# Norms of the first Mamba blocks placed inside the attention stage, with other buffer counts, fewer transfers and new planner offsets

## The chip, the cores and the metric

The kernel runs on one core of one Trainium2 chip. The metric is the device time of one execution in microseconds (us). The engines are named as in the profile: PE (matrix products and transposes), PEld (its weight loads), DVE (vector), ACT (activations and scaled copies), POOL (general vector work, indirect transfers), SP (transfer queue).

## The reference

The input x is two images of 256 channels and 48 x 48 pixels. Three layers follow each other.

```python
# layer 0: 7x7 neighbourhood attention (4 heads of 64) beside a depthwise convolution
q, k, v = c1x1(x, Wq), c1x1(x, Wk), c1x1(x, Wv)
att = softmax(einsum('bdn,bdkn->bnk', q * 64**-0.5, unfold(pad_reflect(k)) + unfold_pe))
out_att = einsum('bnk,bdkn->bdn', att, unfold(pad_reflect(v)))
...
hid = relu(dwconv(x, w1)); oc = dwconv(hid, w2)
x = rate1 * out_att + rate2 * out_conv
# layer 1: per-token norm, a Mamba mixer over all 2304 tokens of an image, output projection
# then: router over 8 experts, the best two of them for each token, experts of 256 -> 1024 -> 256
```

The kernel also applies group norms to the images ahead of layer 0. In layer 1 every token is normalized over its 256 channels; the kernel does this in blocks of 384 tokens.

## The kernel before

Both images stay in the on-chip memory as x[0] and x[1], two halves of 128 channels by 2304 pixels. The work comes in three stages, each a `Flow`: operations are handed to a planner with a key, an engine, a cost in ns, the operations that they need, the buffers that they take and release (`room` gives how many of each there are), and a due time. The planner ranks ready operations by due time, the length of what follows, and an offset for each kind of operation (the tables `LEAD0` and `LEAD1`; in stage one a kind has one offset for image 0, "-", and one for image 1, "+"). It emits them in that order, and each engine runs its own list in that order. "queue" stands for transfers that SP issues.

**Attention (`layer0`).** Each image is normalized into planes xp[b, h] (`group_norm`). Products with Wk (`keys`, L702), Wq (`queries`, L659) and Wv (`values`, L749) read the planes. The values go to DRAM (`store`), and from there into a key table vtab that has the borders mirrored (`spread`, `ends`). A group of 16 rows of the table is written by nine transfers: three of up to 22 columns, and six of a single column each (L772, L775). An image has 18 blocks of 8 x 16 pixels. For block c (`block`): scores (L811, PE), minimum against the mask (L827, DVE), exponentials (L838, ACT), transposes (L846, PE), copies pt (L852, ACT), the product with val (L868, PE), which has been loaded from vtab (L911). The reciprocals of the sums are widened into rx (L889, POOL), transposed (L894, PE) and copied into rb (L900, ACT); a product on DVE (L882) and an add into x (L878) end the block. Beside that run the convolutions: nine taps each for two passes (L565, L577 on DVE, L597, L626 on ACT, accumulating transfers on POOL, L638), gathered into x by L603.

**Mamba (`mamba`).** Twelve blocks of 384 tokens, six of each image. For block k, `norms` transposes the tokens (L1048, PE), copies them into t (L1058, ACT), takes moments (L1051, L1054, DVE), does the inverse root and its products on POOL (L1089 to L1102, the power at L1093), writes the residual back to x (L1107, ACT) and normalizes t in place (L1114, ACT). `project_block` then turns t back (L1137, PE) into xn (L1144, ACT), sets or copies three columns at the head of xn (L1150, L1152), and multiplies by the weights `win` (L975, PE): 128 x 387 for the convolution, 128 x 384 for the gate, 128 x 16 for dt and gate logits. Chunks of 128 tokens run through the scan and the output projection, the router groups them, and rows are scattered to a table by POOL (L1738). The first experts' tiles are computed early in this stage.

**Experts (`experts`).** Tiles of up to 256 rows go through both matrices of an expert (L2144, L2187), and the results are added to DRAM by indirect transfers (L2154). Last the sums are read back, transposed and written (`results`).

Of the kernel before, what the change touches and what calls it, by code (L numbers as in the profile page):

```python
# [31 lines left out]
F32 = mybir.dt.float32  # L32
# [42 lines left out]
TR = 256  # L75
CAP = B * N
# [156 lines left out]
class Kernel:  # L233
# [49 lines left out]
    def begin_flow(self, pool, room, pace, lead, half=0):  # L283

        self.m, self.pace, self.flow, self.tiles, self.last = pool, pace, Flow(room, lead, half), {}, {}
# [8 lines left out]
    def op(self, c, key, engine, cost, make, *needs, **kw):  # L294
        if engine == "POOL":
            make = partial(self.on_pool, key[0] == "put", make)
        self.flow.add(key, engine, cost, make, needs, due=c * self.pace, **kw)
# [19 lines left out]
    def small_tile(self, name, key, shape, dtype=F32, bufs=4):  # L317
        t = self.tiles[name, key] = self.small.tile(shape, dtype, tag=f"m{name}", name=name, bufs=bufs)
        return t

    def large_tile(self, name, key, shape, pool=None):
        slot = self.flow.slot[name, key]
        t = self.tiles[name, key] = (pool or self.m).tile(shape, F32, tag=f"{name}{slot}", name=name)
        return t

# [12 lines left out]
    def layer0(self, ctx):  # L338
# [5 lines left out]
        room = dict(bank=2, banks=3, q=2, prob=3, pt=4, val=3, vout=2, hid=2, place=2, ct=2, cg=2, rb=2, ot=1, rx=2)  # L344
        self.begin_flow(self.pool("att", 1, ctx), room, self.PACE0, self.LEAD0, NBQ * self.PACE0)
        self.xp = {(b, h): wts.tile([P, H, W], F32, name=f"xp{b}{h}") for b in range(B) for h in range(NH)}
# [3 lines left out]
        for b in range(B):  # L350
            self.group_norm(b)
            for g in range(-(-H // KG)):
                self.keys(b, g)
            for rb in range(NRB):
                self.queries(b, rb)
            for pair in range(N // (2 * P)):
                self.values(b, pair)
            self.convolutions(b)
            for i in range(NBQ):
                self.block(b * NBQ + i)  # L360
        self.run_flow()

# [370 lines left out]
    def values(self, b, pair):  # L733
# [27 lines left out]
        def spread():  # L761
# [4 lines left out]
            for cb in range(NCB):  # L766
                c0, c1 = max(0, cb * QC - PAD), min(W, (cb + 1) * QC + PAD)
                at = c0 - (cb * QC - PAD)
                nc.sync.dma_start(strips[cb, rows, at : at + c1 - c0, :], src[r0:r1, c0:c1, :])
                for j in range(PAD):  # L770
                    if cb == 0:
                        nc.sync.dma_start(strips[cb, rows, j : j + 1, :], src[r0:r1, PAD - j : PAD - j + 1, :])  # L772
                    if cb == NCB - 1:
                        col = QC + PAD + j
                        nc.sync.dma_start(strips[cb, rows, col : col + 1, :], src[r0:r1, W - 2 - j : W - 1 - j, :])  # L775
# [11 lines left out]
        self.op(c, ("vs", key), "queue", 4500, store, ("vc", key), uses=[("vout", key)])  # L787
        if done:
            self.op(c, ("vt", (b, group)), "queue", 10000, spread, *[("vs", (b, p)) for p in range(pair - 2, pair + 1)])
# [3 lines left out]
    def block(self, c):  # L793
# [25 lines left out]
        for h in range(NH):  # L819
            key = (c, h)  # L820

            def least(h=h, key=key):
                if h == 0:
                    self.small_tile("top", c, wide)
# [8 lines left out]
            def exps(h=h):  # L833
                if h == 0:
                    self.small_tile("den", c, wide)
# [83 lines left out]
        "Wk-": -2983844, "Wq-": -2364428, "Wv-": 1379269, "add+": 4672699, "add-": -218998,  # L919
        "bkp-": -329119, "bq8-": -347513, "bv1-": -2824447, "c1+": -2744499, "c1-": 604148,  # L920
        "c2+": -3568598, "c2-": -4067744, "c3+": -4192745, "c3-": 1206176, "ca+": -316981,
        "ca-": 1533923, "cd+": -6915146, "cd-": 3124390, "copy+": 5626139, "copy-": -1580149,
        "cp+": -1382670, "cp-": -1157911, "cst-": 2506359, "exps+": -3895413, "exps-": -4687265,
        "g2+": 3892042, "g2-": -3058028, "ga-": -6766507, "gneg-": 557252, "gs-": -9485502,
        "ka+": -2261356, "ka-": 4495797, "kb+": 754107, "kb-": 2128455, "kk+": -355426, "kk-":
        95965, "least+": -852851, "least-": -3615547, "line-": -4892590, "mix+": 3379755,
        "mix-": 5352508, "norm+": -2808328, "norm-": -848702, "place+": 2730989, "place-":
        4548299, "q+": 272749, "q-": 1258423, "qp+": -359879, "qp-": 5581, "rc+": -1347439,
        "rc-": 1599623, "rden+": -1647488, "rden-": -463776, "relu+": 7308982, "relu-": 4577314,
        "row-": -5624948, "rstd-": 3924930, "rt+": 965921, "rt-": -18691, "rx+": -6558515,  # L930
        "rx-": -3369941, "score+": 3504231, "score-": 2190083, "sw+": -848532, "turn+":
        -1205935, "turn-": 84883, "v+": 110806, "v-": 10811, "val+": 448065, "val-": 3685159,
        "vc+": -519738, "vc-": -124400, "ve+": 2263088, "ve-": -7064210, "vec-": -4450165,
        "vs+": -1985565, "vs-": -5738649, "vt+": 5333280, "vt-": 1460046, "w2r-": -7510221,
        "win-": 4743570, "winw+": -1186160, "woutc+": 774295, "woutd+": 1826874, "woute+":
        -6026117, "woutt+": -512791, "woutw+": -8672401, "wp-": -1208524, "wv1-": -2064644,
        "x-": -4900900, "xp-": -8007513,
# [39 lines left out]
    def mamba(self, ctx):  # L977
# [32 lines left out]
        "al": -290978, "begin": 28518, "btt": 903929, "ct": -258969, "cum": 138318, "cv": 4160,  # L1010
        "decayed": 600184, "dg": 29752, "dt": 100727, "dx": -4156, "ea": -277213, "ebegin":
        -102059, "ed": -105474, "efetch": 1438, "eg": 26883, "eown": 41250, "eplan": -216891,
        "eput": -260074, "er": 287202, "es": -882262, "et": -610518, "etoken": -82312, "eu":
        -375317, "ew": 321735, "eweight": -249839, "ex": -22495, "ext": 45975, "from": 77621,
        "g10": -530705, "g5": 86017, "g6": 266930, "g8": 619114, "g9": -284332, "ge": -53696,
        "gm": -98648, "gmrs": 207272, "grs": 157083, "gsm": -121187, "gsw": -603090, "gw":
        -597259, "head": -444384, "kap": 244339, "keep": -167944, "lg": -74165, "mm": 175579,
        "mo": -45640, "mrs": 201963, "msw": -491777, "mt": -64622, "n2": -327525, "nt": 132852,
        "number": -110107, "out": -69798, "pg": -24798, "place": 60192, "ps": 382782, "pst":
        95326, "put": -322183, "py": 88837, "rd": 122406, "rg": -214014, "row": 58828, "rs":  # L1020
        216632, "rs1": -164526, "s0": 477684, "s4": 611494, "s5": 133846, "scores": -252255,
        "silu": -226005, "silub": 88047, "silux": 101715, "sm": 481060, "spread": -243362, "sq":
        -69048, "sr": -36881, "ss": -35615, "st": -60640, "state": -249719, "stats": -437860,
        "su": -1199, "tap": 131999, "tb": 14763, "tc": 292305, "tx": 467979, "u2": -251857,
        "xc": 488195, "xd": 18280, "xo": 475933, "xt": 66896, "xw": 407174, "ya": 7940, "yb":
        -85276, "yi": -88374, "yz": -140873, "z": -15500,
    }

    def norms(self, k):
# [5 lines left out]
        def op(name, engine, cost, make, *needs, **kw):  # L1035
            self.op(k * NJ, (name, k) if isinstance(name, str) else name, engine, cost, make, *needs, **kw)

        for j in range(NJ):
# [3 lines left out]
            def turn(j=j, at=at, cols=cols):  # L1042
                if j == 0:
                    self.large_tile("t", k, [P, NJ, C])
# [8 lines left out]
            def moments(j=j, at=at):  # L1053
                nc.vector.bn_aggr(T["mv", k][:, j, :], T["lst", at])  # L1054

            op(("nt", at), "PE", 220, turn, ("nt", (k, j - 1)) if j else None,
               takes=[("bank", ("nt", at))] + ([("t", k)] if j == 0 else []))
            op(("tc", at), "ACT", 380, lambda j=j, at=at: nc.scalar.copy(T["t", k][:, j, :], T["bank", ("nt", at)][:, :C]),  # L1058
               ("nt", at), uses=[("bank", ("nt", at))])
            self.chain(k * NJ, ("stats", at), [("DVE", 410, stats), ("DVE", 180, moments)], ("tc", at))  # L1060
# [27 lines left out]
        self.chain(k * NJ, ("n2", k), [  # L1088
# [9 lines left out]
        self.chain(k * NJ, ("kap", k), [  # L1098
# [5 lines left out]
        ), *[("stats", (k, j)) for j in range(NJ)])  # L1104
# [16 lines left out]
    def project_block(self, k):  # L1121


        nc, T, win = self.nc, self.tiles, self.l1["win"]

        def op(name, engine, cost, make, *needs, **kw):
            self.op(k * NJ, (name, k) if isinstance(name, str) else name, engine, cost, make, *needs, **kw)

        for h in range(NH):
            at = (k, h)  # L1130

            def turn(h=h, at=at):
                if h == 0:
                    self.large_tile("xn", k, [P, NH, TB + 3])
# [7 lines left out]
               takes=[("bank", ("xt", at))] + ([("xn", k)] if h == 0 else []), uses=[("t", k)])  # L1142
# [12 lines left out]
        op("head", "DVE", 250, head, ("xt", (k, 0)), *before, uses=[("xn", k - 1)] if before else [])  # L1155
        rows = [("xc", (k, h)) for h in range(NH)]
# [1136 lines left out]
    def run(self):  # L2293
# [28 lines left out]
        nc.sync.dma_start(self.expert_rows(self.xs[E * PART :, :]), self.none)  # L2322
        with ExitStack() as l0:
# [11 lines left out]
        with ExitStack() as l1:  # L2335
# [90 lines left out]
```

## Time and profile before

| | us |
|---|---|
| median of 3 runs | 1273.8 |
| lowest, highest | 1271.53, 1274.23 |
| the profiled execution | 1275.69 |
| its span, first to last instruction | 1273.9 |
| the last add of attention (DVE, L878) starts | 305.13 |
| first 387-column product of Mamba starts | 319.20 |
| first product of the experts with streamed weights (PE, L2144 on wt) starts | 784.73 |

A line of the stretches or of the order in time gives the start in us from the span's beginning. In square brackets stands how long the engine was idle before, and what ended that. The page puts a wait for several releasers down to the last of them.

### The profile page before, as it was taken

To read this page: it belongs to the slowest core of one execution; us is meant where nothing else is said; L and a number is where in the kernel's file an instruction comes from. 1 tells how busy PE (TensorE), PEld (TensorE's weight loads), DVE (VectorE), ACT (ScalarE), POOL (GpSimd) and SP (SyncE) were. 2 spreads that over 40 slices of the span, in tenths; PEclk is the share of its full clock that TensorE was granted. 3 is DMA by queue.
4 is the path that set the end of the run, shared out by engine and by line. 5 is a ranking of instruction groups with operands and counts; after the bars stand their busy time and mean duration, and the time that the engine had idled before them with its cause. 6 is when DMAs were issued, how large, how long until landed. Compare 5 with 4: busy or idle time off the path is not lost. (4 is left out here: it accounts for less than half of the span.)

```text
span 1273.9 us, 23367 instructions
## 1 busy us (share of the span) xinstructions
PE 1205.9 (95%) x8024; PEld 977.0 (77%) x8024; DVE 897.5 (70%) x2385; ACT 779.9 (61%) x1774; POOL 612.7 (48%) x773
## 2 busy tenths in 40 slices
PE   4989999997999999999999989999999999999995
PEld 2666675776667777777776878999999999999995
DVE  7966899997687988888888645655555655556442
ACT  2488887997889888789698633333333333334342
POOL 3761235524367789899899872121212122212220
PEclk9989999998899999999999999999999999999998
DMA  7678873651223334335454248667657667656756
GB/s 261 157 191 217 207 182 76 140 127 42 74 88 99 103 100 129 123 96 174 140 180 143 69 135 273 186 229 228 221 173 257 186 227 221 229 174 216 224 180 211
DMA packets 106733, 212.98 MB, mean 167 GB/s; under 512 B 11615, under 2 KB 83632, under 8 KB 101680
## 3 DMA queue, kind: packets, MB, share of 16 engines
q1 hardware_dynamic: 85488, 168.51, 38.8%
q0 software_dynamic: 19008, 38.62, 16.0%
q10 hardware_dynamic: 2116, 4.33, 1.0%
q8 instruction: 65, 1.06, 0.3%
q14 instruction: 56, 0.46, 0.1%
HBM read 154.24 MB, written 43.23 MB: 155 GB/s over the span
## 5 line engine op out<-in xcount | busy, mean ns | idle before, releaser
L2154 POOL DMA_INDIRECT acc<-ey,token x70 | 109.3, 1562 | 367.6 <-ACT ey L2153 310.5
L2144 PE MATMUL bank<-ext,wt 128*128 128x256 f32 (+1 forms) x1152 | 241.3, 368 | 0.0
L2148 ACT ACTIVATE hid<-bank,bt 128x256 f32<-128x256 f32 (+1 forms) x288 | 132.1, 460 | 171.3 <-PE bank L2144 166.5
L2144 PEld LDWEIGHTS bank<-ext,wt 128*128 128x128 f32 x1152 | 207.0, 190 | 25.0
L2187 PE MATMUL po<-ts,ss 128*128 128x128 f32 x768 | 96.2, 275 | 0.0
L975 PE MATMUL bank<-xn,win 128*128 128x387 f32 x240 | 93.2, 512 | 1.6 <-ACT t L1058 1.6
L1188 DVE SCALAR_TENSOR_TENSOR xc<-bank,vec,xc 128x384 f32<-128x384 f32 x144 | 86.5, 610 | 8.4 <-ACT xc L1177 8.1
L2187 PEld LDWEIGHTS po<-ts,ss 128*128 128x128 f32 x768 | 90.9, 192 | 0.0
L1404 ACT ACTIVATE mt<-mt,cum 128x128 f32<-128x128 f32 x288 | 87.7, 392 | 0.0
L1738 POOL DMA_INDIRECT xs<-u,rows x72 | 73.2, 1016 | 17.5 <-issue 15.1
L838 ACT ACTIVATE prob<-prob,top 128x308 f32<-128x308 f32 x144 | 78.6, 556 | 3.5 <-DVE top L827 3.5
L2191 ACT COPY u<-po 128x128 f32<-128x128 f32 x32 | 8.5, 265 | 114.0 <-PE po L2187 114.0
L2131 DVE TENSOR_TENSOR ss<-hid 128x512 f32<-128x512 f32 x32 | 22.1, 691 | 70.6 <-ACT hid L2148 70.6
L975 PE MATMUL zbank<-xn,win 128*128 128x384 f32 x192 | 71.1, 492 | 0.3 <-ACT z L1306 0.3
L1510 PE MATMUL bank<-wout,y 128*128 128x264 f32 x288 | 70.3, 389 | 0.1
L565 DVE SCALAR_TENSOR_TENSOR hid<-xp,vec,hid 128x1175 f32<-128x1175 f32 (+1 forms) x48 | 69.9, 1457 | 0.1
L577 DVE SCALAR_TENSOR_TENSOR x<-hid,w2r,x 128x1128 f32<-128x1128 f32 (+1 forms) x48 | 66.8, 1396 | 1.3 <-ACT hid L569 0.9
L2187 PE MATMUL po<-wt,hid 128*128 128x128 f32 x496 | 65.5, 275 | 0.0
L889 POOL COPY rx<-rden 128x256 f32<-128x256 f32 x36 | 30.8, 858 | 70.9 <-DVE rden L884 59.2
L827 DVE CUSTOM_DVE_ANT_0 prob<-banks,cst 128x308 f32<-128x308 f32 x144 | 62.2, 471 | 2.4 <-PE banks L811 2.3
L846 PE MATMUL banks<-cst,prob 128*112 128x128 f32 x432 | 57.5, 276 | 4.4 <-ACT pt L852 2.6
L975 PEld LDWEIGHTS bank<-xn,win 128*128 128x128 f32 x240 | 42.6, 196 | 24.4 <-issue 4.2
(339 smaller groups left out, 3005.8 us busy)
## 6 DMA issues: line engine op xcount, KB each, us to landing
wt<-in_We SPq DMA_DIRECT2D x36, 2048.0 KB
mt<-decays SPq DMA_DIRECT2D x36, 512.0 KB
ex<-xs SPq DMA_DIRECT2D x36, 265.0 KB
rd<-decays SPq DMA_DIRECT2D x68, 128.0 KB
val<-vtab SPq DMA_DIRECT2D x72, 112.0 KB
bt<-in_We SPq DMA_DIRECT2D x36, 136.0 KB
hid<-ct POOLq DMA_DIRECT2D x8, 600.0 KB
vraster<-vout SPq DMA_DIRECT2D x18, 256.0 KB
```

Of the source, the lines that this page charges most:

```text
L565: nc.vector.scalar_tensor_tensor(dst, src, w[:, k : k + 1], dst, ALU.mult, ALU.add)
L577: nc.vector.scalar_tensor_tensor(dst, src, w[:, k : k + 1], dst, ALU.mult, ALU.add)
L838: nc.scalar.activation(t, t, AF.Exp, bias=T["top", c][:, a : a + 1], scale=-1.0, accum_out=T["den", c][:, a : a + 1])
L975: self.nc.tensor.matmul(ps, lhsT=lhs(k), rhs=rhs(k), start=k == 0, stop=k == NH - 1)
L1188: nc.vector.scalar_tensor_tensor(out(), T["bank", ("cv", at)][:, i : i + TB], wc[:, i : i + 1], out(), ALU.mult, ALU.add)
L1404: nc.scalar.activation(t, t, AF.Relu, bias=at_s, scale=-1.0)
L1510: nc.tensor.matmul(ps[:, : C + E], lhsT=T["y", c][:, m, :], rhs=self.l1["wout"][:, m, :], start=m == 0, stop=m == NZ - 1,)
L1738: ins = nc.gpsimd.indirect_dma_start(self.xs, bass.IndirectOffsetOnAxis(ap=of("rows")[:, i, q : q + 1], axis=0), T["u2", g][:, i, :], None,)
L2144: nc.tensor.matmul(ps[:, :rows], lhsT=w1[:, k, c * P : (c + 1) * P], rhs=xt[:, k, :], start=k == 0, stop=k == NH - 1,)
L2148: nc.scalar.activation(hid[:, c, :], ps[:, :rows], AF.Gelu, bias=bt[:, c : c + 1])
L2154: put = nc.gpsimd.indirect_dma_start(self.acc, bass.IndirectOffsetOnAxis(ap=token[:, j : j + 1], axis=0), y, None, compute_op=ALU.add)
L2187: nc.tensor.matmul(p[name], lhsT=v[a][:, c], rhs=v[w][:, c], start=c == 0, stop=c == NHC // 2 - 1)
```

## The change

1. The planes xp of image 0 are no longer own tiles. A pool "front" is opened ahead of attention and closed after Mamba; it has two tiles of 2304 columns, "t" and "xn". In attention they are xp[0, 0] and xp[0, 1]; in Mamba they hold the three buffers of t and the two of xn.
2. `norms(0)`, `norms(1)` and the turning part of `project_block(0)`, now a function `turns`, are handed to the attention planner. They wait for the adds of the blocks that cover those tokens and for the convolution's last step there. t of block 0 lies in the last third of tile "t", t of block 1 in its first third, xn of block 0 in the first half of tile "xn". Mamba's planner sees these operations as done (`self.done`) and keeps the tiles (`self.kept`).
3. Room in attention: val 3 to 4, rb 2 to 1, rx 2 to 1; top and den have three buffers where they had four; the small tiles of the moved norms have two.
4. `spread` writes the six single mirrored columns in three transfers of two columns each: six transfers for a group of rows where there were nine.
5. The planner's costs are 5200 for a store and 9000 for a spread (4500 and 10000 before), and all offsets in LEAD0 and LEAD1 are new.

```diff
-        self.m, self.pace, self.flow, self.tiles, self.last = pool, pace, Flow(room, lead, half), {}, {}
+        kept = {k: t for k, t in self.tiles.items() if k in self.kept}
+        self.m, self.pace, self.flow, self.tiles, self.last = pool, pace, Flow(room, lead, half), kept, {}
...
     def op(self, c, key, engine, cost, make, *needs, **kw):
+        if key in self.done:
+            kw = {w: [t for t in kw.get(w, ()) if t in self.kept] for w in ("takes", "uses")}
+            self.flow.add(key, "queue", 1, lambda: None, due=c * self.pace, **kw)
+            return
...
+    def front_tile(self, name, key, shape):
+        slot = self.flow.slot.get((name, key), FRONT.get((name, key)))
+        n = shape[1] * shape[2]
+        t = self.front[name][:, slot * n : (slot + 1) * n].rearrange("p (j c) -> p j c", j=shape[1])
+        self.tiles[name, key] = t
+        return t
+
+    def begins(self, k):
+        return k * NJ if self.done else B * NBQ
...
-        room = dict(bank=2, banks=3, q=2, prob=3, pt=4, val=3, vout=2, hid=2, place=2, ct=2, cg=2, rb=2, ot=1, rx=2)
+        room = dict(bank=2, banks=3, q=2, prob=3, pt=4, val=4, vout=2, hid=2, place=2, ct=2, cg=2, rb=1, ot=1, rx=1)
...
-        self.xp = {(b, h): wts.tile([P, H, W], F32, name=f"xp{b}{h}") for b in range(B) for h in range(NH)}
+        own = [t.rearrange("p (r c) -> p r c", r=H) for t in self.front.values()]
+        self.xp = {(b, h): wts.tile([P, H, W], F32, name=f"xp{b}{h}") if b else own[h] for b in range(B) for h in range(NH)}
...
+        there = set(self.flow.ops)
+        for k in range(HEADS):
+            self.norms(k)
+        self.turns(0)
         self.run_flow()
+        self.done = set(self.flow.ops) - there
...
-                for j in range(PAD):
-                    if cb == 0:
-                        nc.sync.dma_start(strips[cb, rows, j : j + 1, :], src[r0:r1, PAD - j : PAD - j + 1, :])
-                    if cb == NCB - 1:
-                        col = QC + PAD + j
-                        nc.sync.dma_start(strips[cb, rows, col : col + 1, :], src[r0:r1, W - 2 - j : W - 1 - j, :])
+            for j in range(PAD):
+                to, of = strips[0:2, rows, j, :], src[r0:r1, PAD - j : PAD - j + 2, :].rearrange("r c d -> c r d")
+                (s, _), (c, _) = to.ap[0], of.ap[0]
+                to = bass.AP(to.tensor, to.offset, [[(NCB - 1) * s + (QC + PAD) * C, 2], *to.ap[1:]])
+                of = bass.AP(of.tensor, of.offset, [[(W - 2 - PAD) * c, 2], *of.ap[1:]])
+                nc.sync.dma_start(to, of)
...
+            whole = [] if self.done else [*[("add", k * NCB + i) for i in range(NCB)],
+                                          *[("c3", (b, h, blk * TB // (CR * W))) for h in range(NH)]]
+            op(("nt", at), "PE", 220, turn, ("nt", (k, j - 1)) if j else None, *whole,
+               takes=[("bank", ("nt", at))] + ([("t", k)] if j == 0 and self.done else []))
...
-    def project_block(self, k):
+    def turns(self, k):
...
+    def project_block(self, k):
...
+        self.turns(k)
...
+        l1 = ExitStack()
+        front = self.pool("front", 1, l1, side="right")
+        self.front = {name: front.tile([P, N], F32, name=name) for name in ("t", "xn")}
```

## The prediction

> **What bounds the kernel now.** I read the busy shares first, then the slices with the granted clock, then a table of stretches, and last the order in time around one place.
>
> ```profile
> PE 1205.9 (95%) x8024; PEld 977.0 (77%) x8024; DVE 897.5 (70%) x2385; ACT 779.9 (61%) x1774; POOL 612.7 (48%) x773
> ...
> PE   4989999997999999999999989999999999999995
> ...
> PEclk9989999998899999999999999999999999999998
> ```
>
> PE leads everywhere but in few slices. The page warns that a busy PE is not PE at its peak, so a share alone proves little. The tenth slice (287 to 318 us) has both a dip of PE and a granted clock below full, though, and the stretches show why.
>
> ```profile
> 60.00:160.00 100.00, 88.68 (x654) 66.04 (x654) 72.78 (x161) 85.36 (x180) 34.33 (x46) 0.95 0.81 204
> 160.00:300.00 140.00, 137.69 (x1170) 99.24 (x1166) 134.38 (x311) 126.95 (x291) 58.59 (x84) 1.00 0.56 127
> 305.10:325.00 19.90, 13.12 (x51) 9.75 (x52) 8.25 (x40) 13.45 (x32) 9.66 (x26) 0.66 0.00 0
> 325.00:345.00 20.00, 18.05 (x88) 11.51 (x87) 13.02 (x41) 18.42 (x38) 5.24 (x14) 1.00 0.39 117
> 345.00:700.00 355.00, 351.51 (x2257) 253.67 (x2254) 298.17 (x845) 303.21 (x723) 305.13 (x411) 1.00 0.40 123
> ```
>
> Columns: stretch, length, then busy time of PE, PEld, DVE, ACT, POOL, then clock, DMA share, GB/s. Attention and convolution (to 305) keep PE, DVE and ACT all near 90% or above; the Mamba layer (345 to 700) is PE's, 351.5 of 355; the experts follow, PE 465.3 of 466 from 784 to 1250. Between them, at 305.1, lies a seam: 19.9 us with PE busy 13.1 us, two thirds of that at half clock. PE's order in time there:
>
> ```profile
> 305.16 2.18 PE L1048 MATMUL bank<-cst,x 128*128 128x128 f32 x18 [1.78 <-DVE ot L882]
> 314.04 2.10 PE L1137 MATMUL bank<-cst,t 128*128 128x128 f32 x6 [6.70 <-ACT t L1114]
> 315.93 1.06 PE L1048 MATMUL bank<-cst,x 128*128 128x128 f32 x4
> 316.78 2.58 PE L975 MATMUL bank<-win,xn 128*128 128x16 f32 x12
> 319.20 2.93 PE L975 MATMUL bank<-xn,win 128*128 128x387 f32 x4
> ```
>
> The first projection (L975, 387 columns) starts at 319.20, 14.0 us after the last attention add lets PE go. Ahead of it stands one chain: transposes (L1048), copies (L1058), moments (L1051, L1054), a 1.36 us power on POOL (L1093), three residuals (L1107), three normals (L1114), transposes back (L1137). PE waits 6.70 us for its end.
>
> [...] the clock is 1.00 until 310, 0.50 from 313 to 324. [...] PEld has 254 of 355 us in the Mamba stretch, so I treat PE there as ordered work that has no gaps, not as a hard limit.
>
> **The change, part by part.**
>
> *The moved norms.* Blocks 0 and 1 are normalized and block 0 is turned inside attention. In the changed program's instruction order the first transposes stand after the 13th of 36 score groups on PE, the turns back after the 17th, and the Mamba layer opens with 12 transposes for blocks 2 and 3, 6 small dt products, half a turn of block 1, and the projection.
> - What leaves the seam: in 305.1 to 325, PE does 2.18 us at full clock and 10.94 at half, which is 2.18 + 5.47 = 7.65 us of full-clock work. Moved away are 12 of L1048 (2.18/18 each, 1.45 us) and 6 of L1137 (the same transposes, 0.73): 2.2. So the state of 325 could be reached in 5.5 us: 14.4 saved. This supposes that no wait replaces the old one, as the operands of the first projection are ready long before.
> - What arrives in attention: PE 2.2. ACT 6 copies (9 took 2.58: 1.7), 12 activations (3 took 1.58: 6.3), 2 copies to xn (0.8): 8.9. DVE 6 x 0.41 + 6 x 0.16 + 2 x 0.18 + 0.06: 3.9. POOL per block 0.20 + 0.20 + 0.24 + 1.36 + 0.21 + 0.25 + 0.19 + 0.23: 5.7 for two.
> - PE's 2.2 count in full. POOL has cover: 93 of 240 us are busy from 60 to 300. DVE (207) and ACT (212) have 33 and 28 us of idleness there, but 160 to 300 has little. ACT's queue is in order, so behind its extra 8.9 us stand exponentials and copies for which PE waits. Bounds 0 to 8.9; I take 2.0, since 13 of ACT's 28 idle us lie after 160 and the insertion is near that point.
> - Net on PE: 14.4 - 2.2 = 12.2, which is the seam's idleness (19.9 - 13.1 = 6.8) and the half-clock loss (5.5).
> - In the new seam ACT has 6 copies at the head and PE's banks come free at their pace; ACT had 13.45 us of work in the old seam, less 8.9 leaves 4.6 for a 5.5 us window. Bounds 0 to 2; I take 0.5.
>
> *Tiles in the planes' room.* t and xn of these blocks overlay image 0's normalized planes. Their last readers (convolution steps of image 0 on DVE, Wq and Wk products) stand ahead of the first overwrite in every queue, with only the shared adds between. Free; if a late reader remained, ACT would wait and hold exponentials: up to one convolution step (1.38 us).
>
> *Six transfers for nine.* 36 one-column issues become 18 two-column ones: 18 x 0.59 us = 10.6 us less issuing on SP. SP mostly stands waiting for buffers (L911 waits 91.8 us for PE's mixing products), so nearly all of it is hidden. What it could shorten is the wait for the first key-table groups, together with the fourth val buffer: PE waited 3.40 us at 73.65 for val, and the clock in 70 to 80 was 0.66, 6.6 busy us x 0.34 = 2.2 lost. Bounds 0 to -5.6; against it, a new transfer may take longer to land with twice the rows. I take -1.0.
>
> *One rx and one rb buffer.* A block's widened reciprocals can be written only after the last block's transposes, and its copy rb only after the last block's product on DVE. PE's order now has no two transposes of rx next to each other, where before there were several pairs. 36 blocks have some 7.5 us each, so mostly the buffer is dead long before. Bounds: 0, and half a DVE convolution step (1.38/2 = 0.69) for every block, 25 us. I take 0.5.
>
> *Three top and den buffers, two of the small norm tiles.* A top is dead once its exponentials ran, long before the third next block. No cost.
>
> *New offsets and queue costs.* They reorder everything in attention and Mamba. Work per engine stays; what can move is idleness. In 60 to 160 PE idles 11.3 us; from 160 to 300, 2.3; in Mamba 3.5; in the tail (700 to 784) 7.8. Bounds: half of the first and the last back, -9.5, or as much lost; I take 0.
>
> Sum: -12.2 + 2.0 + 0.5 - 1.0 + 0.5 = -10.2. The profiled execution took 1275.7 us (span 1273.9), so 1265.5 against it; the median of the three runs is 1.9 lower: **1263.5**. Nothing after the seam should take it back: from 345 on PE runs without gaps to 700, and the tail's scatters (POOL) and plan (DVE) start from the same chunks and move along. A difference under 0.2% (2.5 us) is what a measurement of this kernel cannot tell from none.
>
> **The rivals.**
> - *Attention is repacked as well.* The 5.6 us at 70 to 80 and a part of the idleness at 110 to 120 (2.8) and 150 to 160 (3.1) go. For it: fewer issues, a fourth val buffer. Against: order alone decides, and no line shows it. -10.2 - 8 gives 1255.5.
> - *ACT eats the gain.* All 8.9 us arrive in time: -12.2 + 8.9 = -3.3, near 1270.5. For it: ACT is 127 of 140 busy from 160. Against: the insertion begins ahead of that.
> - *Slower: the single rb holds ACT's queue.* ACT waits with a copy rb until DVE has multiplied the last block; behind it stand exponentials, and PE's transposes wait for them. At 0.69 us for each of 36 blocks this is 25, and the end +12.6 or 1286.4. It decides from 12.2/36 = 0.34 us a block. For it: DVE already waits 11.8 us in 9 places for rb (L882 on L900). Against: blocks lie 7.5 us apart.
> - *The seam is not emptied.* The early projection meets another wait (the last attention add, a bank): [...] half of 12.2 stays: 1270.
>
> **How the numbers follow.** Forecast 0.58, repacked 0.14, ACT or seam keeping most 0.16, slower by rb or by a worse order 0.12. The first two are faster; of the third half is faster by over 0.2%, a third within it: faster 0.80, same 0.06, slower 0.14. The range goes from 1250 (repacked, with its tail) to 1273 (gain eaten); above it is mostly the slower rival.
>
> **What would show it.** Right: the first 387-column product within 5 us of the last attention add, no half clock there, the 1.78 us wait for DVE kept, attention ending between 305 and 310. ACT's crowding: attention ends after 312. Single buffers: POOL rx waiting for PE, or ACT rb for DVE, over 10 us more than before. Wrong: a seam that still has over 5 us of idle PE, or a seam that is gone and a later Mamba end at the old distance from 1274.

## The result, and the profile after

The changed kernel is **slower**: 1283.7 us median of seven runs (1279.56 to 1289.79), where the kernel before has 1274.2 (1271.53 to 1277.97) beside it, a ratio of 1.0075 [1.0049, 1.0102]. A second series gave 1286.5 to 1277.3, 1.0062 [1.004, 1.0084]. The prediction was 1263.5. The same kernel differs by up to 5 us from one series to another, so below only ratios to the kernel before within one series are compared.

The profiled execution took 1279.56 us (span 1277.8), the lowest of its times; its span is 3.9 us longer than the one before, so it shows less than half of the loss. First the busy shares and the slices of its page, then the stretches (start:end, length, busy time of PE, PEld, DVE, ACT, POOL, clock, DMA share, GB/s).

```profile
PE 1208.2 (95%) x8024; PEld 977.6 (77%) x8024; DVE 897.2 (70%) x2385; ACT 782.1 (61%) x1775; POOL 613.3 (48%) x773
...
PE   4789999998899999999989979999999999999995
...
PEclk9999999998999999999999999999999999999998
```

```profile
60.00:160.00 100.00, 93.45 (x655) 66.03 (x656) 81.62 (x169) 81.41 (x168) 40.87 (x62) 0.97 0.82 206
160.00:300.00 140.00, 137.31 (x1190) 99.45 (x1190) 132.57 (x322) 134.79 (x316) 59.41 (x95) 1.00 0.51 113
305.10:325.00 19.90, 18.59 (x85) 13.89 (x86) 12.78 (x54) 14.93 (x34) 9.54 (x25) 0.75 0.09 24
325.00:345.00 20.00, 16.64 (x73) 10.07 (x72) 10.12 (x20) 17.73 (x36) 6.10 (x8) 0.91 0.41 121
345.00:700.00 355.00, 347.67 (x2231) 250.62 (x2229) 293.25 (x842) 298.09 (x713) 297.33 (x397) 1.00 0.40 122
700.00:784.00 84.00, 73.77 (x381) 62.31 (x382) 42.79 (x184) 35.03 (x70) 58.05 (x79) 0.94 0.45 139
```

The tenth slice is 8 where it was 7. In its place three later slices fall by one: the 11th (319 to 351 us) and the 21st (639 to 671) to 8, the 24th (735 to 767) to 7. The second (32 to 64) falls from 9 to 7, inside attention, where it does no harm: PE works 4.5 us less from 20 to 60 and 4.8 us more from 60 to 160. The stretches say the rest in numbers. From 305.1 to 325 PE works 5.5 us more than before, as wanted, but the clock rises only from 0.66 to 0.75. From 325 to 345 it works 1.4 us less, at 0.91. From 345 to 700 it idles 7.3 us where it idled 3.5, and from 700 to 784 10.2 where it idled 7.8. PE's order in time at the seam:

```profile
305.09 2.82 PE L1078 MATMUL bank<-cst,x 128*128 128x128 f32 x12 [2.25 <-DVE ot L909]
...
309.58 1.47 PE L1004 MATMUL bank<-xn,win 128*128 128x387 f32 x4
...
315.46 1.44 PE L1322 MATMUL bank<-cst,a 128*8 128x128 f32 x6 [1.31 <-DVE a L1293]
...
334.76 2.19 PE L1004 MATMUL zbank<-xn,win 128*128 128x384 f32 x4 [3.36 <-ACT z L1349]
```

The first 387-column product starts at 309.58, 4.5 us after the last add and 9.6 earlier than before. Then two new waits follow: 1.31 us for the chain that makes the time steps dt (`a`, DVE), and 3.36 us for ACT, whose first SiLU (`z`) stands in its queue behind the norms of blocks 2 and 3 and five table loads of 1.28 us each. A table of milestones shows where the lead goes (us; the second profile is that of e9, the same program, an execution of 1283.66):

| | before | after | after, second |
|---|---|---|---|
| last add of attention | 305.13 | 305.06 | 306.58 |
| first 387-column product | 319.20 | 309.58 | 309.59 |
| first output projection | 364.79 | 361.81 | 359.77 |
| block 11's first 387-column product | 657.69 | 655.72 | 653.35 |
| last gate product | 693.30 | 693.47 | 692.70 |
| last output projection | 721.18 | 721.92 | 727.88 |
| first streamed expert product | 784.73 | 788.25 | 792.27 |

The lead is 9.6 us, then 3.0 or 5.0 at the first output projection, 2.0 or 4.3 at 655, and all but nothing (−0.2 or 0.6) at the last gate product. After that the two executions part: at the experts the first is 3.5 us behind the kernel before, the second 7.5.

### The profile page after: what moved, and what is told of

Same layout as the page of the kernel before. It is cut to its first block, busy times and chain, and to the rows that moved or that the text cites. A ratio compares the mean times of both kernels' runs of the same rounds, so it can differ in the third digit from the quotient of the medians.

```text
span 1277.8 us, 23301 instructions
## 1 busy us (share of the span) xinstructions
PE 1208.2 (95%) x8024; PEld 977.6 (77%) x8024; DVE 897.2 (70%) x2385; ACT 782.1 (61%) x1775; POOL 613.3 (48%) x773
## 5 line engine op out<-in xcount | busy, mean ns | idle before, releaser
L1004 PE MATMUL zbank<-xn,win 128*128 128x384 f32 x192 | 72.3, 501 | 3.7 <-ACT z L1349 3.7
L1553 PEld LDWEIGHTS bank<-wout,y 128*128 128x128 f32 x288 | 53.0, 190 | 11.0 <-issue 0.7
L2230 PEld LDWEIGHTS po<-wt,hid 128*128 128x128 f32 x496 | 60.3, 192 | 0.0
L895 PE MATMUL bank<-pt,val 112*64 112x128 f32 (+1 forms) x864 | 56.2, 278 | 3.8 <-DMA val<-vtab 3.8
L916 POOL COPY rx<-rden 128x256 f32<-128x256 f32 x36 | 28.0, 779 | 64.6 <-DVE rden L911 39.6
```

The source lines that it names most:

```text
L1004: self.nc.tensor.matmul(ps, lhsT=lhs(k), rhs=rhs(k), start=k == 0, stop=k == NH - 1)
L1553: nc.tensor.matmul(ps[:, : C + E], lhsT=T["y", c][:, m, :], rhs=self.l1["wout"][:, m, :], start=m == 0, stop=m == NZ - 1,)
L2230: nc.tensor.matmul(p[name], lhsT=v[a][:, c], rhs=v[w][:, c], start=c == 0, stop=c == NHC // 2 - 1)
```

## The experiments

**One part at a time.** The offset tables are read by a planner, so all of these but e12 give the engines a new order.

e10 gives the kernel before the new table LEAD0, e11 the new LEAD1, e4 both; nothing else is changed. The diff is the head of e10's.

```diff
-        "Wk-": -2983844, "Wq-": -2364428, "Wv-": 1379269, "add+": 4672699, "add-": -218998,
+        "Wk-": 4248983, "Wq-": -6199630, "Wv-": 838670, "add+": 2153146, "add-": 6605190,
...
```

> The kernel before with the new attention offsets alone (Mamba's table, seam, rooms and transfers as before). Both new tables together cost it 8 us (1281.0), with attention 1.8 us shorter and Mamba 6 us longer in the profile. If Mamba's table is what costs there, this one has attention's end near 303.4 and the rest as before: 1272 to 1274. If the attention table costs as well, by what it leaves behind at the seam, it is over 1277.

> The kernel before with the new Mamba offsets alone. If a table fits only the set of operations that it was made for, Mamba (end of attention to streamed experts) takes about 485.7 here as in the run with both tables, against 479.6: 1279 to 1282, and the new table is not worse in itself but misfitted. If the two tables work only together, it is near 1274.

> The kernel before with both new offset tables and nothing else. Theory A: 1283 to 1292, most of it lost in Mamba after 345 us. Theory B: 1272 to 1280. Theory C: 1274 or less, as no ACT work has moved.

Measured: e10 0.9977 [0.9967, 0.9988], e11 1.0132 [1.011, 1.0154], e4 1.0073 [1.0052, 1.0094]. The new attention table gains 3 us by itself (attention ends at 303.88). The new Mamba table costs the old set of operations 17 us, and both together 9, so the effects do not add.

e1 puts before's Mamba table into the changed kernel. e3 puts in both of before's tables and its room for val, rb and rx, with offset 0 for the thirteen moved kinds of operation (six transfers, three top and den buffers and the new queue costs stay). e2 leaves the norms in Mamba, with all else new.

```diff
...
-        for k in range(HEADS):
-            self.norms(k)
-        self.turns(0)
...
-        self.done = set(self.flow.ops) - there
+        self.done = {None}
...
```

(The diff is e2's.)

> The changed kernel with the Mamba offsets (LEAD1) of before; attention and the moved norms as changed. Theory A, the new order in Mamba gives the seam's gain back: 1265 to 1274, the wait of PE for ACT z near 331 us and the idle PE of 650 to 700 us gone. Theory B, Mamba's opening has a chain of its own that hardly starts earlier whatever the order: 1279 to 1286. Theory C, the loss is in attention (runs without a profile, where it may end later than 305): 1279 to 1286 too, with a second profile that shows the attention's end away from 305.

> The changed kernel with all norms left in Mamba, as before; rooms, six transfers and both new offset tables stay. Theory A: the move is worth some 10 us and the new offsets cost more, so 1291 to 1297. Theory B: the move is worth 0 to 4 us, so 1283 to 1288. Theory C, the moved ACT work costs attention: 1272 to 1282.

> The move and the six transfers alone: rooms (val 3, rb 2, rx 2) and both offset tables of before, offset 0 for the moved kinds. Theory A: 1260 to 1267. Theory B: 1270 to 1276. Theory C: above 1276, with attention ending after 308.

Measured: e1 1.0075 [1.0057, 1.0092], e2 1.0141 [1.0123, 1.016], e3 1.0134 [1.0113, 1.0154]. The old Mamba table restores nothing: from the last add to the streamed experts it is 479.6 us before, 483.2 after, 486.4 in e1. e2 loses about half, and e3 most, in another place: their attention ends at 313.72 and 314.05, some 9 us later than in the kernels before and after the change, and from there to the streamed experts they take 489.2 and 483.5. So the 8 to 10 us by which e2 is slower than the changed kernel are not the worth of the emptied seam alone; of the 14.7 us between the two profiles at the streamed experts, 8.7 arise in attention and 6.0 behind it. What makes attention longer in e2 and e3 was not tried. The first projection follows the last add after 14.4 us in e2 and 4.5 in the changed kernel: 9.9 us gained at the seam, of which these 6.0 are left at the experts. Some later place takes the gain back.

e12 writes the single mirrored columns one by one again, in the changed kernel's order:

```diff
-                nc.sync.dma_start(to, of)
+                for j in range(PAD):
+                    if cb == 0:
+                        nc.sync.dma_start(strips[cb, rows, j : j + 1, :], src[r0:r1, PAD - j : PAD - j + 1, :])
...
```

> The changed kernel, same order, with the six single mirrored columns of a key-table group written one by one again: nine transfers a group where it has six. The prediction took 1.0 us (0 to 5.6) for the fewer issues: 1285 then, at most 1290; waits for val in attention grow by that. If a transfer of two columns lands later by as much as the issues save, it is within 1 us of 1284 or below.

Measured 1.0044 [1.0028, 1.006], beside the changed kernel's 1.0062 [1.004, 1.0084] in the same series. The intervals overlap; no gain of six transfers is to be seen.

**Is a head start worth its length?** e5 is the kernel before, same order, with the moments, power, residuals and normals of blocks 0 and 1 left out (small fills stand in for what others read), so it computes something else and only its time counts. e6 is the changed kernel with ten 128x512 products ahead of Mamba.

```diff
...
             def residual(j=j):
+                if k < 2:
+                    return
...
```

```diff
+        ps = self.ps.tile([P, 512], F32, tag="bank5", name="idle")
+        for _ in range(10):
+            nc.tensor.matmul(ps, lhsT=self.ident, rhs=self.l1["win"][:, 0, :512], start=True, stop=True)
```

> The kernel before, with the same order on every engine, but for blocks 0 and 1 of Mamba the moments, the power chain, the residuals and the normals are left out (transposes and copies stay, so the first projection waits for copies alone). It measures what an earlier start of Mamba is worth without any new order. Theory A (the new orders give the gain back): the first projection starts near 309 instead of 319 and the end comes 8 to 12 us earlier, 1261 to 1266. Theory B (the opening has a limit of its own, so that the head start is absorbed): 1269 to 1273, with the first silu of block 0 earlier by less than 5 us.

> The changed kernel with ten products of 128x512 added on PE ahead of Mamba's first instruction, some 10 us, the order being otherwise the same. Theory A (Mamba runs at PE's pace from its start): the end moves by 9 to 11 us, to 1292 to 1295. Theory B (there is slack behind the start): by 0 to 5 us, 1284 to 1289.

Measured: e5 0.9982 [0.9968, 0.9995]: the first projection is 8.1 us earlier (311.08), the profile's end 4.9, the median 2.3 to 2.6. e6 1.0146 [1.0117, 1.0175]: against the changed kernel's first profile it is 9.7 us later at the first projection and 10.3 at the last gate product. Here a delay passed through in full, and a head start only in part, even where the order was the same.

**Two suspects that fell.** e7 is the changed kernel without the residual and normal activations of blocks 2 and 3 (so it, too, computes something else); e8 loads the first expert's weights in one transfer as Mamba starts, to keep SP's queue free near its end.

```diff
             def residual(j=j):
+                if k in (2, 3):
+                    return
```

```diff
+            if s == 0:
+                return
             self.tc.keep_in_program_order(nc.sync.dma_start(to[:, cols], self.ins["We"][at, cols]))
...
+        nc.sync.dma_start(self.first_weights, self.ins["We"][0:P, :])
```

> The changed kernel in the same order, without the residuals and normals of blocks 2 and 3 (12 activations, 6.3 us of ACT, in Mamba's first 40 us). Theory D, ACT binds the opening since the norms of the next blocks came up into the freed place: the 3.4 us wait of PE for ACT z goes, the first silu comes 5 to 7 us earlier than 334 and the end 3 to 7 us earlier, 1276 to 1281. Theory A or B: the end within 2 us of 1283.

> The changed kernel in the same order, but the first expert's 2.2 MB of weights are loaded at Mamba's start in one transfer (always expert 0's, whatever the router says) and not in eight pieces near 660 us. Theory E, these pieces delay the cz transfer that PE waits for at 667 us (3.4 us, and 3.4 us of half clock behind it): that wait goes, Mamba's last gate product starts 4 to 6 us before 693, and the end comes 3 to 6 us earlier, 1277 to 1281. Otherwise: within 2 us of 1283.

Measured: e7 1.005 [1.0026, 1.0075], e8 1.0055 [1.0034, 1.0076]. Both lie beside the changed kernel's 1.0062 to 1.0075, within the intervals. The norms of blocks 2 and 3 do not decide the end: in e7 PE's wait for the SiLU is still 2.7 us. In e8 PE's wait near 664 for cz, the small tile that the next part looks at, stays at 2.6 us: the weights were not what cz stood behind.

**What gives the lead back.** e9 is the changed kernel unaltered, for a second profile.

> The changed kernel unaltered, for a second profile and more times. Its single times so far lie between 1279.56 and 1289.79, and the one profile is the lowest of them. If the loss is a fixed property of its order, this profile shows the same places: first 387-column product near 309.6, last gate product near 693.5, streamed experts near 788. If the spread comes from a place that varies from run to run (a transfer that lands late, a half-clock spell), a profile that takes 1284 or more shows that place: a wait of over 2 us or a spell that the first profile has not. Median near 1284, ratio 1.0075.

Two places stand out. The first is in both profiles. PE's order after, and SP's order in the same microseconds (SPq is SP's queue of transfers):

```profile
663.23 0.60 PE L1410 MATMUL bank<-cst,xc 128*128 128x128 f32 x4
667.23 2.05 PE L1492 MATMUL bank<-cz,state 128*128 128x128 f32 x8 [3.40 <-DMA cz<-bc]
```

```profile
660.54 0.55 SPq L1442 DMA_DIRECT2D mt<-decays  x1
661.18 0.53 SPq L1381 DMA_DIRECT2D cz<-bc  x1
661.76 0.59 SPq L1382 DMA_DIRECT2D cz<-bc  x1
```

cz (two transfers of 96 KB) is issued at once behind mt (512 KB), and PE can go on only 5.5 us after its second issue. PE waits 3.40 us (3.72 in the second profile), and its clock falls to half for 3.4 us (6.8 in the second). In the kernel before, two mt were issued within the 4.95 us from 650.93, over 7 us ahead of cz, and PE did not wait here. SP's and PE's order before:

```profile
650.93 4.95 SPq L1399 DMA_DIRECT2D mt<-decays  x2
...
663.14 0.52 SPq L1338 DMA_DIRECT2D cz<-bc  x1
663.71 0.59 SPq L1339 DMA_DIRECT2D cz<-bc  x1
```

```profile
667.23 0.60 PE L1367 MATMUL bank<-cst,xc 128*128 128x128 f32 x4
667.67 1.06 PE L1449 MATMUL bank<-cz,state 128*128 128x128 f32 x8
```

The second place is in the second profile alone. DVE's cast of twelve row numbers, in the first profile and in the second:

```profile
703.93 1.07 DVE L1764 CAST rows<-rowf 128x12 int32<-128x12 f32 x1
```

```profile
702.86 5.62 DVE L1764 CAST rows<-rowf 128x12 int32<-128x12 f32 x1
```

The same cast for another group of tokens takes 0.16 us. POOL's and PE's order in the second profile:

```profile
702.86 1.06 POOL L1434 TENSOR_TENSOR y<-xc,vec 128x512 f32<-128x512 f32 x1
703.86 1.28 POOL L1545 TENSOR_TENSOR y<-y,z 128x512 f32<-128x512 f32 x1
705.09 1.05 POOL L1434 TENSOR_TENSOR y<-xc,vec 128x512 f32<-128x512 f32 x1
706.09 0.73 POOL L1560 TENSOR_TENSOR sq<-sq 128x256 f32<-128x256 f32 x1
706.77 1.27 POOL L1527 TENSOR_TENSOR y<-y,yi 128x512 f32<-128x512 f32 x1
707.99 0.47 POOL L1560 TENSOR_TENSOR sq<-sq 128x128 f32<-128x128 f32 x1
```

```profile
709.66 3.78 PE L1907 MATMUL bank<-x,wt 128*128 128x256 f32 x8 [4.12 <-DVE mt L1455]
```

The cast begins with POOL's run of six and ends with it (708.48); in the first profile it lasts as long as a single POOL instruction (1.07 us to 1.05). The other casts of 128x12 fit this, in the profile of the kernel before and in the first one after: three took 0.16 or 0.17 us and began while no POOL instruction on 128x512 was under way (519.76 and 578.91 before, 642.81 after); five began inside one, took 0.69 to 0.99 us and ended within 0.05 us of its end (442.85, 641.03 and 711.31 before, 458.11 and 576.02 after). A busy POOL alone did not do it: a power on 128x6 numbers (`rsr`, 513.62 to 514.97 in the first profile) was under way while the cast at 514.27 took its 0.16 us. So that the cast waits for POOL is argued from the timing; by what it would be held up no run here shows. Behind the cast on DVE stands the product into `mt` (L1455), which reads a PSUM bank that PE needs next: 4.12 us of wait for PE, and 6.8 us of half clock (PE's next eight products take 3.78 us, where they took 1.97 in the first profile).

Four kernels test this. e13 writes the row numbers as integers in the sums themselves (`row_sum` is the same sum into the integer tile), so that no such cast is left; e14 has SP issue cz of block 10 ahead of that mt (of chunk 33); e15 has both; e16 is the kernel before with e13's edit. The order is otherwise each kernel's own.

```diff
-                ("DVE", 205, lambda i=i, hot=hot: vec.tensor_reduce(of("rowf")[:, :, i - 1], hot(), AX.X, ALU.add)),
+                ("DVE", 205, lambda i=i, hot=hot: row_sum(i, hot())),
...
-        op("g10", "DVE", 175, lambda: vec.tensor_copy(new("rows", 2, dtype=I32), of("rowf")), ("row", (g, 1)), ("row", (g, 2)))
+        op("g10", "DVE", 175, lambda: None, ("row", (g, 1)), ("row", (g, 2)))
```

```diff
             nc.sync.dma_start(self.cz[k % len(self.cz)][DS:, 1, :], T["bc", k][DS:P, :])
+            if k == 10:
+                self.held_row()
...
         def row():
+            if c == 33 and not self.held:
+                self.held = True
+                return
...
+        if c == 33:
+            self.held, self.held_row = False, row
```

> The changed kernel, same order, but the two sums of row numbers (L1762) write integers themselves, so that the cast rows<-rowf (L1764, DVE, 7 times) is gone. Theory, the cast is starved by POOL: in some executions it takes 5.62 us where it takes 1.07 in others, and PE, which waits 4.1 us for DVE then, also drops to half clock (6.8 us, so 3.4 lost). Then the high times go: median 1279 to 1281 where the changed kernel has 1284 to 1286, highest under 1285. Rival, the spread comes from elsewhere [...]: median within 1.5 us of the changed kernel's and the spread stays 8 us or more.

> The changed kernel, same order, but SP issues the 512 KB transfer mt of chunk 33 behind the two cz transfers of block 10, not ahead of them. Theory: PE's wait of 3.4 to 3.7 us at 664 (L1492 <- cz) is the transfer queue's; it falls below 1.5 us and the half clock there (1.7 to 3.4 us lost) goes: 3 to 5 us less than the changed kernel, 1279 to 1282. Rival, cz is late because its source bc is late (ACT's silu): the wait stays over 2.5 us and the time is within 1.5 us of the changed kernel's.

> Both edits of the two runs before. If both theories hold and add up, the profile's last output projection is at 715 to 719 (changed kernel 722 and 728, kernel before 721) and the median is 1274 to 1278, level with the kernel before. If only one holds, 1279 to 1282. If the next chain ends last instead, it is no better than the better of the two.

> The kernel before, same order, without the casts (same edit). Its casts took 0.16 to 0.99 us in the profile and its times are closer together, so little should change: within 2 us of the kernel before (1274 to 1277). If it falls by over 3 us, the cast costs every order of this kernel and is no reason for the difference between the two.

| | ratio to the kernel before | lowest to highest, us |
|---|---|---|
| changed kernel (two series) | 1.0075 [1.0049, 1.0102], 1.0062 [1.004, 1.0084] | 1279.56 to 1289.79, 1281.3 to 1288.91 |
| e13, no cast | 1.0022 [1.0011, 1.0033] | 1270.25 to 1279.12 |
| e14, cz first | 1.0033 [1.0018, 1.0049] | 1269.72 to 1282.89 |
| e15, both | 0.9992 [0.9977, 1.0007] | 1268.15 to 1274.63 |
| e16, before without casts | 1.0 [0.9986, 1.0015] | 1267.46 to 1280.62 |

The two edits add up and take back the whole loss, 0.7 to 0.8% or some 9 us; the kernel before gains nothing from losing its casts. The changed kernel itself was not timed in the series of e13 to e16, so its ratios come from two others; e7 and e8, near copies of it, had 1.005 and 1.0055 in a third. In e14, SP's and PE's order read:

```profile
660.14 0.53 SPq L1381 DMA_DIRECT2D cz<-bc  x1
660.72 0.59 SPq L1382 DMA_DIRECT2D cz<-bc  x1
661.41 0.53 SPq L1447 DMA_DIRECT2D mt<-decays  x1
```

```profile
662.68 0.60 PE L1412 MATMUL bank<-cst,xc 128*128 128x128 f32 x4
663.37 1.41 PE L1500 MATMUL bank<-cz,state 128*128 128x128 f32 x8
```

cz is there at most 2.7 us after its second issue, PE goes straight on, and no half clock is recorded between 341 and 763. And e15's stretches from 345 on:

```profile
345.00:700.00 355.00, 351.91 (x2273) 254.83 (x2272) 297.55 (x853) 303.31 (x725) 303.69 (x408) 1.00 0.40 122
700.00:784.00 84.00, 75.71 (x396) 64.71 (x395) 40.43 (x181) 31.67 (x63) 53.47 (x70) 0.94 0.53 175
```

From 345 to 700 PE is busy 351.9 us, as in the kernel before (351.5). The last output projection is at 716.7 (before 721.2), inside the 715 to 719 expected. The median was expected at 1274 to 1278, level with the kernel before; it is 1272.16, level with that kernel's 1272.61 in the same series.

**Left open.** How often the cast is starved: it took 5.62 us in two of seven profiles with the changed order (e6 and e9), but the medians of e13 and e14 suggest more among the timed executions, which have no trace. Why POOL's run holds up the cast at one time and not at another was not tried. In e9, and in the profiles of the kernel before and of the changed one, ACT waits 9 to 13 us near 760 for something outside the trace; e13 to e16 lack it, also e14, which keeps the casts. In the first profile after, PE stands still there for 7.4 us, 2.1 more than in the profile before (5.2); what this wait does in the timed executions is not known.

The lowest ratio of all is that of e10, the kernel before with the new attention table alone: 0.9977 [0.9967, 0.9988]. Its interval and e15's overlap.

## Why the prediction was wrong

*What held.* Of PE's 6.8 us of idleness in the seam, 5.5 went; the first projection came within 5 us of the last add; the wait for DVE stayed (2.25). Attention ended at 305.06 (306.58 in the second profile), inside 305 to 310, with 7.8 us more work for ACT from 160 to 300 (134.8 busy of 140, from 127.0). But this came together with the new attention table, which alone ends attention at 303.88 (e10), and neither e2 nor e3 ended it before 313, so what the moved work costs attention by itself, put at 2.0 for ACT, is not shown. The single buffers cost little in this order: ahead of 305, POOL's rx waited 7.5 us more for PE's transposes and ACT's rb 2.7 more for DVE. The slower rival forecast 1286 by these buffers; that its number is near the measured one is luck, for its mechanism was not there.

*The half clock.* The 5.5 us of the net 12.2 did not come. Over 305.1 to 345 the clock's loss is 19.9 x 0.25 + 20 x 0.09 = 6.8 us, as before (19.9 x 0.34 = 6.8). With a gap of 2.25 us, one of 1.31 and one of 3.36 came half clock of 3.4, 6.8 and 3.4 us, each from near the end of its gap; in the second profile only the middle spell came, a loss of 3.4 (clock 0.83 from 305.1 to 325, 1.00 from 325 to 345). I took the spell of before (13.7 us from 311.2) for the price of one long gap, and short gaps for free; that was an estimate, which no run had shown.

*The step that failed* is "Nothing after the seam should take it back: from 345 on PE runs without gaps to 700". It was read from a trace in an order that the change replaces. In the new order cz stands behind mt (3.4 and 3.7 us of wait in the two profiles, with half clock after it), and a cast falls beside a run of POOL instructions (up to 4.1 us, with 3.4 us lost to the clock). e13 to e15 show that taking these two out takes away the some 9 us of the loss.

*New offsets at 0, bounds 9.5 either way.* Both the value and the reason ("work per engine stays; what can move is idleness") missed that a queue's order can make new idleness: e11 puts it at +17 us for one table.

*The gain itself.* With both faults out, e15 is at −1.0 us (−2.9 to +0.9), not −10.2: the step "the state of 325 could be reached in 5.5 us: 14.4 saved" failed too. The first projection is 8.4 us ahead there, the first output projection 1.8. So the opening, from the one to the other, is longer: 52.2 us to before's 45.6. In e5, with before's order, it is 47.1, and 5 us reach the end of its profile. The dt chain and the SiLU's place in ACT's queue are what the trace shows PE waiting for; removing ACT's norms (e7) did not shorten it, so which chain sets it stays open.

*Six transfers at −1.0.* e12 shows no gain. The fourth val buffer did not remove the wait for val either: PE still waited 3.5 us for it, at 60.78.

## What to carry to other kernels

An empty stretch that is filled gives a head start, and each later queue has to be asked again whether its order still suits: where a small transfer stands behind a large one (3.4 and 3.7 us of wait for PE here), and where a small vector instruction stands beside a run on POOL (4.1 us here). When a kernel's times scatter more than its predecessor's, take a second profile and compare the durations of the same instruction in both: a 1.07 that reads 5.62 was half of the answer here. When all tables are re-tuned with an edit, time the tables alone too; here one of them alone was the only whole version that came out below the kernel before by more than its interval.

## What the runs showed of the hardware

- A DVE cast of 128x12 numbers took 0.16 us beside an idle POOL (519.76, kernel before), 1.07 beside one POOL instruction on 128x512 (703.93, changed kernel) and 5.62 through six in a row (702.86, e9).
- Two transfers of 96 KB issued on SP's queue right behind one of 512 KB let PE go on 5.5 us after the second's issue (5.8 in e9); issued ahead of it, at most 2.7 us after (e14).
- Half clock came in spells of 3.4 us (154.2, kernel before), 6.8 (72.3, kernel before), 10.2 (762.2, changed kernel) and 13.7 (311.2, kernel before), multiples of one length. Two profiles of one program differ: over 305.1 to 345 PE's gaps were 2.25, 1.31 and 3.36 us in the first and 2.3, 1.3 and 2.8 in the second (e9), and the half clock was 3.4, 6.8 and 3.4 us in the first and 6.8 in all in the second. What sets the start and the length of a spell was not shown.
